# The softmax sums of layer 0 in four streams of 32 columns

## The chip, the cores and the metric

The kernel runs on one core of a Trainium2 chip. The metric is the device time of one execution in microseconds. "Before" is the median of three executions. One further execution was recorded by the hardware profiler, and every duration of a single instruction comes from that one.

The engines are named as in the profile: PE is TensorE (matmul), PEld its weight loads, DVE VectorE, ACT ScalarE, POOL GpSimd, and SP the engine whose queue issues most of the transfers. PSUM is the memory into which PE writes its results; a bank holds 512 f32 values in each of 128 partitions. SBUF is the working memory.

## What is computed

Two attention layers follow each other on `x` of shape (8, 512, 32, 32): 8 batches, 512 channels, 1024 tokens, 8 heads of 64 channels. Only layer 0 is touched. Cut to what matters:

```python
normed = group_norm(x)                                # 32 groups
q, k, v = split(qkv_w @ normed + qkv_b)               # each 8 heads x 64 x 1024
weight = einsum('bct,bcs->bts', q * scale, k * scale) # scores
weight = softmax(weight, axis=-1)
a = einsum('bts,bcs->bct', weight, v)
out = proj_w @ (normed_in + a) + proj_b
x = x + out
```

The kernel doesn't divide each weight. It takes `e = exp(scores)` and multiplies `e` with `v`, sums `e` over the keys, and multiplies the result by the reciprocal of that sum at the end. The sums are what the change is about.

## The kernel before

**How the work is cut.** The order of all instructions on all engines is written out by hand; nothing is rearranged by a scheduler, and each engine works its own list in order. Layer 0 goes through the batches one by one. For a batch, `attention0` works through 8 groups: 4 pairs of heads times 2 halves of 512 queries. A group has `NG` = 8 blocks of 128 keys, so there are 64 steps `i` for a batch.

- `scores(i)` (line 972): four 64x64 matmuls of 512 columns into a PSUM tile of two banks, then `exp` on ACT (line 977) into `e[i]`, a tile of 128 partitions by 2 x 512. The partitions are the 128 keys of the block, the middle index `m` is the head of the pair.
- `values(i)` (line 998): products of `e` with `v`, summed over the 8 blocks in two PSUM banks, tags `a0` (two buffers) and `a1`. After the last block ACT copies both to `u[g]` (line 1009).
- `sums(i)` (lines 983 and 985): DVE adds `e[i]` to `zacc[g]`, of the same shape. After the last block, `zacc[g]` still has 128 partial sums for each query and head, one in each partition.

The loop takes two steps at a time: `scores` of i and i + 1, then `values` and `sums` of i - 2 and i - 1, then what an agenda has for the slots i and i + 1. For a group whose last block has just been done, the agenda gets `totals(g)` at slot i + 2, `reciprocals(g)` at i + 6 and `finish(g)` at i + 10. Group 7 of a batch comes too late for the loop; its three steps run in `ag.flush()`, after the next batch's k projection (`qk0(b + 1, "k")`) has been issued, or at the end of the layer for the last batch.

**The steps that the change touches.**

- `totals(g)` (line 1011) adds the 128 partial sums by a matmul with a matrix of ones. It does so for the upper and the lower 64 partitions apart: half `a` goes into `z[a]`, `z[0]` in a buffer of tag `a0`, `z[1]` in the bank `small`. Each of the four matmuls is 64 rows by 64 columns and streams 512 columns. Then ACT copies `z[0]` and DVE `z[1]` to `row`, and SP issues two transfers that bring one row of each head into `zc[g]`, laid out over 128 partitions with 8 values each.
- `reciprocals(g)` (line 1031) adds the two halves of the values `u[g]`, adds the two halves of the sums into `zs` (line 1035), takes the reciprocal, writes it to a DRAM tile `zd`, and reads it back spread over 64 partitions for each head as `rzb[g]` (line 1042). It also keeps a record in `chk` for a later test of the range.
- `finish(g)` (line 1056) multiplies `u[g][0]` by `rzb[g]` (line 1058) and adds it to `xa` (line 1060), the input of the output projection.

The bank `small` has a second user: the group statistics of the next batch. `gs.means` (line 616) copies the means on DVE into `gs_m` (line 618) and multiplies them on PE into `pm` (line 620) in `small`. It is due at slot 43, directly behind `totals(4)` at slot 42; `finish(3)` is due at slot 42 too, ahead of `totals(4)`. `gs.squares` follows at slot 45 (line 631). This happens for batches 0 to 6, each preparing the next.

After the flush of group 7 come the v and q projections of the next batch (lines 846 and after), which use the `a0` buffers as well; for the last batch comes the output projection, of which the last part needs `finish(7)`.

Layer 1 has a `totals` of its own (line 1567, matmul at line 1574), which isn't changed. It sums over all 128 partitions at once, in four streams of 32 columns:

```python
nc.tensor.matmul(
    ps[c * 32 : c * 32 + 32, m].rearrange("p (g c i) -> p g c i", g=4, i=Q8),
    ones[:, :32],
    self.by_head(z[:, c // 2])[:, c % 2 * 4 : c % 2 * 4 + 4],
    start=True, stop=True, tile_position=(0, c * 32),
)
```

Of the kernel before, what the change touches and what calls it, by code (L numbers as in the profile page):

```python
# [9 lines left out]
F32 = mybir.dt.float32  # L10
# [8 lines left out]
P = 128  # L19
# [448 lines left out]
def tile_two_attention_layers(  # L468
# [19 lines left out]
    nc = tc.nc  # L488
    B, C, T = x_d.shape
    H = w_head.shape[0]  # L490
    D = C // H
    NCC = C // P
    NT = T // P
    FB = 512
# [21 lines left out]
    def const_tile(name, shape, dt=F32):  # L516
        return const.tile(shape, dt, tag=name, name=name)
# [13 lines left out]
    ones = const_tile("ones", [P, P])  # L531
# [118 lines left out]
    with ExitStack() as l0:  # L650
# [4 lines left out]
        zpool = l0.enter_context(tc.tile_pool(name="zpool", bufs=2))  # L655
        stat = l0.enter_context(tc.tile_pool(name="stat", bufs=2))
        ps_s = l0.enter_context(tc.tile_pool(name="ps_s", bufs=2, space=PSUM))
        ps_a = l0.enter_context(tc.tile_pool(name="ps_a", bufs=1, space=PSUM))

        def small_psum(nm):  # L660
            return ps_a.tile([P, FB], F32, tag="small", name=nm)

        def score_psum(nm):
            return ps_s.tile([P, 2, FB], F32, tag="s", name=nm)
# [295 lines left out]
        def attention0(b, agenda):  # L960
            q, k, v = q_t[b], k_t[b], v_t[b]
            e, acc, u, zacc, zc, rzb = {}, {}, {}, {}, {}, {}

            def scores(i):

                f, hp, kc = i // (NG * H // 2), i // NG % (H // 2), i % NG
                ps = score_psum(f"s0_{b}_{i}")
                for c in range(2):
                    for m in range(2):
                        r = slice(m * D, m * D + D)  # L970
                        k0 = kc * P + c * D
                        nc.tensor.matmul(  # L972
                            ps[c * D : c * D + D, m], k[r, hp, k0 : k0 + D], q[r, hp, ts(f, FB)],
                            start=True, stop=True,
                        )
                e[i] = epool.tile([P, 2, FB], F32, tag="e", name=f"e0_{b}_{i}")
                nc.scalar.activation(e[i], ps, AF.Exp, scale=S0 * S0)  # L977

            def sums(i):
                g, kc = i // NG, i % NG  # L980
                if kc == 1:
                    zacc[g] = zpool.tile([P, 2, FB], F32, tag="zacc", name=f"zacc_{b}_{g}")
                    nc.vector.tensor_add(zacc[g], e[i - 1], e[i])
                elif kc > 1:
                    nc.vector.tensor_add(zacc[g], zacc[g], e[i])  # L985

            def values(i):

                g, hp, kc = i // NG, i // NG % (H // 2), i % NG
                if kc == 0:  # L990
                    acc[g] = [
                        ps_a.tile([P, FB], F32, tag=f"a{a}", name=f"a0_{b}_{g}_{a}", bufs=2 - a)
                        for a in range(2)
                    ]
                for a in range(2):
                    rows = slice(a * D, a * D + D)
                    for m in range(2):
                        nc.tensor.matmul(  # L998
                            acc[g][a][m * D : m * D + D], v[rows, kc, ts(2 * hp + m, D)],
                            e[i][rows, m], start=(kc == 0), stop=(kc == NG - 1),  # L1000
                        )
                if kc == NG - 1:

                    u[g] = [
                        zpool.tile([P, FB], F32, tag=f"u{a}", name=f"u_{b}_{g}_{a}")
                        for a in range(2)
                    ]
                    for a in (1, 0):
                        nc.scalar.copy(u[g][a], acc[g][a])

            def totals(g):

                z = [
                    ps_a.tile([P, FB], F32, tag="a0", name=f"z_{b}_{g}", bufs=2),
                    small_psum(f"z_{b}_{g}_1"),
                ]
                for a in range(2):
                    rows = slice(a * D, a * D + D)
                    for m in range(2):
                        nc.tensor.matmul(  # L1020
                            z[a][m * D : m * D + D], ones[rows, :D], zacc[g][rows, m],
                            start=True, stop=True,
                        )
                row = zpool.tile([P, 2, FB], F32, tag="row", name=f"row0_{b}_{g}", bufs=1)
                nc.scalar.copy(row[:, 0], z[0])
                nc.vector.tensor_copy(row[:, 1], z[1])
                zc[g] = stat.tile([P, 2, T // P], F32, tag="zc", name=f"zc_{b}_{g}")
                for a in range(2):
                    nc.sync.dma_start(out=zc[g][:, a], in_=row[0::D, a])

            def reciprocals(g):

                nc.vector.tensor_add(u[g][0], u[g][0], u[g][1])
                zs = stat.tile([P, T // P], F32, tag="zs", name=f"zs_{b}_{g}")
                nc.vector.tensor_add(zs, zc[g][:, 0], zc[g][:, 1])
                rz = stat.tile([P, T // P], F32, tag="rz0", name=f"rz_{b}_{g}")
                nc.vector.reciprocal(rz, zs)
                zd = dram.tile([2, FB], F32, tag=f"zd0_{b}_{g}", name=f"zd0_{b}_{g}")
                nc.sync.dma_start(out=zd, in_=rz)
                rzb[g] = zpool.tile([P, FB], F32, tag="rzb", name=f"rzb_{b}_{g}")  # L1040
                for m in range(2):
                    nc.sync.dma_start(
                        out=rzb[g][m * D : m * D + D], in_=zd[m].partition_broadcast(D)
                    )
                col = b * H + g
                junk = stat.tile([P, T // P], F32, tag="junk0", name=f"junkz_{b}_{g}")
                nc.vector.tensor_scalar(
                    junk, zs, 1.0, 0.0, ALU.mult, ALU.add, accum_out=chk[:, 1, col : col + 1]
                )
                r2 = stat.tile([P, T // P], F32, tag="r20", name=f"r2_{b}_{g}")  # L1050
                nc.vector.scalar_tensor_tensor(
                    r2, rz, 1.0 / RZ_MAX, rz, ALU.mult, ALU.mult,
                    accum_out=chk[:, 0, col : col + 1],
                )

            def finish(g):
                hp, f = g % (H // 2), g // (H // 2)
                nc.vector.tensor_mul(u[g][0], u[g][0], rzb[g])
                dst = xa_t[b][:, hp, ts(f, FB)]
                nc.vector.tensor_add(dst, dst, u[g][0])  # L1060


            for i in range(0, NI + 2, 2):
                if i < NI:
                    scores(i)
                    scores(i + 1)
                if i >= 2:
                    for w in (i - 2, i - 1):
                        values(w)
                        sums(w)  # L1070
                    if (i - 1) % NG == NG - 1:
                        g = (i - 1) // NG
                        agenda.at(i + 2, lambda g=g: totals(g))
                        agenda.at(i + 6, lambda g=g: reciprocals(g))
                        agenda.at(i + 10, lambda g=g: finish(g))
                agenda.run(i)
                agenda.run(i + 1)
# [55 lines left out]
    with ExitStack() as l1:  # L1133
# [8 lines left out]
        zpool = l1.enter_context(tc.tile_pool(name="zpool1", bufs=1))  # L1142
        stat = l1.enter_context(tc.tile_pool(name="stat1", bufs=2))
        gstat = l1.enter_context(tc.tile_pool(name="gstat", bufs=1))
        ps_a = l1.enter_context(tc.tile_pool(name="ps1_a", bufs=1, space=PSUM))
# [583 lines left out]
        for b in range(B):  # L1729
            more = b + 1 < B  # L1730
            a = Attention1(b)
# [105 lines left out]
```

## Time and profile before

| | us |
|---|---|
| median of three executions | 4401.87 |
| lowest, highest | 4401.12, 4406.87 |
| the profiled execution's own time | 4397.52 |
| its span in the trace | 4395.7 |
| `zacc` sums' matmul, line 1020: 512 instructions, duration of one | 0.589 |
| copy of `z[0]` on ACT, line 1025: 64, duration of one | 0.586 |
| copy of `z[1]` on DVE, line 1026: 64, duration of one | 0.692 |
| issue of a transfer `zc`, line 1029: 128, duration of one | 0.555 |
| add of the halves, line 1035: 64, duration of one | 0.160 |

A matmul on f32 data appears as two instructions in the trace, so 64 calls with four matmuls give 512. Matmuls on different parts of the array run beside each other, and their ends are modelled. So their durations can't be added up; how long a block of matmuls holds PE is read from the start of its first instruction to the start of the next block's first one. In a timeline each line has the start, the length from the first start to the last end, engine, line, operation, result and operands, sizes, and how many instructions were merged. What stands in brackets is how long the engine had been idle before, and what ended that.

Layer 0 takes the first 1,790 us or so of the span; the rest is layer 1.

### The profile page before, as it was taken

To read this page: it belongs to the slowest core of one execution; us is meant where nothing else is said; L and a number is where in the kernel's file an instruction comes from. 1 tells how busy PE (TensorE), PEld (TensorE's weight loads), DVE (VectorE), ACT (ScalarE), POOL (GpSimd) and SP (SyncE) were. 2 spreads that over 40 slices of the span, in tenths; PEclk is the share of its full clock that TensorE was granted. 3 is DMA by queue.
4 is the path that set the end of the run, shared out by engine and by line. 5 is a ranking of instruction groups with operands and counts; after the bars stand their busy time and mean duration, and the time that the engine had idled before them with its cause. 6 is when DMAs were issued, how large, how long until landed. Compare 5 with 4: busy or idle time off the path is not lost.

```text
span 4395.7 us, 131459 instructions
## 1 busy us (share of the span) xinstructions
PE 4251.2 (97%) x58752; PEld 2266.0 (52%) x58752; DVE 2690.5 (61%) x3683; ACT 2330.0 (53%) x2747; POOL 53.4 (1%) x86
## 2 busy tenths in 40 slices
PE   7999999999999999899999999999999999999998
PEld 4353535353535353366466466466466465465565
DVE  4748484848484847268367377277277277376387
ACT  1717172727272725078177177187187286286385
POOL 0000000000000000000000000000000000000000
PEclk9999999999999999899999999999999999999999
DMA  4112121211111111277186176275285384384474
GB/s 134 59 57 70 58 69 58 69 63 66 64 63 65 62 56 38 77 184 182 54 200 165 65 197 157 77 196 146 89 196 134 97 206 117 113 198 108 115 175 134
DMA packets 249311, 487.13 MB, mean 111 GB/s; under 512 B 58592, under 2 KB 63072, under 8 KB 244512
## 3 DMA queue, kind: packets, MB, share of 16 engines
q1 hardware_dynamic: 243856, 475.84, 39.2%
q8 instruction: 462, 7.57, 0.7%
q0 software_dynamic: 2576, 0.69, 0.3%
q10 hardware_dynamic: 2304, 2.10, 0.1%
q14 instruction: 113, 0.93, 0.1%
HBM read 167.53 MB, written 41.42 MB: 48 GB/s over the span
## 4 chain that ended last, share of the span: by engine, by line
PE 89%; DVE 4%; DMA 3%; ACT 2%; issue 2%; SPq 0%; DVEq 0%; ACTq 0%
PE a L1543 11%; PE s L1449 11%; PE m L1497 10%; PE s L972 9%; PE a L998 9%; PE pk L1248 5%; PE pv L1272 5%; PE pq L1304 5%; PE pp L1334 4%; PE pp_p L846 4%; PE pv_p L846 4%; PE pk_p L846 4%; PE pq_p L846 4%; PE t L1574 2%; DMA re<-raw 1%
## 5 line engine op out<-in xcount | busy, mean ns | idle before, releaser
L1497 PEld LDWEIGHTS m<-wmix,re 64*64 64x64 f32 x32768 | 581.3, 135 | 130.8 <-issue 64.2
L1497 PE MATMUL m<-wmix,re 64*64 64x64 f32 x32768 | 594.0, 219 | 32.0 <-issue 25.8
L977 ACT ACTIVATE e<-s 128x1024 f32<-128x1024 f32 x512 | 497.2, 1026 | 229.8 <-PE s L972 229.8
L1543 PE MATMUL a<-e,v 128*64 128x256 f32 x4096 | 558.8, 392 | 25.6 <-ACT q L1565 21.0
L1521 DVE TENSOR_TENSOR z<-z,e 128x1024 f32<-128x1024 f32 x448 | 537.2, 1218 | 54.5 <-ACT e L1503 54.4
L1525 DVE TENSOR_TENSOR z<-z,e 128x1024 f32<-128x1024 f32 x448 | 534.5, 1218 | 57.6 <-ACT e L1514 56.8
L1503 ACT ACTIVATE e<-m 128x1024 f32<-128x1024 f32 x512 | 528.5, 1032 | 74.3 <-PE m L1497 70.8
L1449 PE MATMUL s<-k,q 64*64 64x256 f32 x8192 | 550.6, 387 | 4.9 <-issue 4.9
L972 PE MATMUL s<-q,k 64*64 64x512 f32 x4096 | 487.5, 591 | 2.3 <-ACT e L977 2.3
L985 DVE TENSOR_TENSOR zacc<-zacc,e 128x1024 f32<-128x1024 f32 x384 | 468.0, 1219 | 26.9 <-ACT e L977 2.3
L998 PE MATMUL a<-e,v 64*64 64x512 f32 x4096 | 484.1, 589 | 0.0
L1514 ACT ACTIVATE e<-e 128x1024 f32<-128x1024 f32 x448 | 461.9, 1062 | 0.0
L1464 ACT COPY raw<-s 128x1024 f32<-128x1024 f32 x368 | 373.8, 1016 | 149.8 <-PE s L1449 118.4
L1449 PEld LDWEIGHTS s<-k,q 64*64 64x64 f32 x8192 | 268.2, 132 | 266.8 <-issue 172.8
L1543 PEld LDWEIGHTS a<-e,v 128*64 128x64 f32 x4096 | 251.1, 136 | 146.4 <-ACT q L1565 24.3
L998 PEld LDWEIGHTS a<-e,v 64*64 64x64 f32 x4096 | 156.6, 133 | 282.9 <-issue 282.9
L972 PEld LDWEIGHTS s<-q,k 64*64 64x64 f32 x4096 | 152.9, 133 | 283.2 <-issue 259.4
L1462 DVE COPY raw<-s 128x1024 f32<-128x1024 f32 x144 | 176.2, 1223 | 109.1 <-PE s L1449 98.0
L1248 PE MATMUL pk<-y,wk 128*128 128x512 f32 x512 | 230.3, 604 | 4.4 <-DMA y<-x 4.4
L1312 ACT COPY q<-pq 128x512 f32<-128x512 f32 x32 | 18.8, 586 | 396.5 <-DVE q L1314 396.5
L1272 PE MATMUL pv<-wv,y 128*128 128x512 f32 x512 | 227.6, 598 | 0.0
L1304 PE MATMUL pq<-y,wq 128*128 128x512 f32 x512 | 221.1, 592 | 0.0
(261 smaller groups left out, 3766.5 us busy)
## 6 DMA issues: line engine op xcount, KB each, us to landing
re<-raw SPq DMA_DIRECT2D x1024, 256.0 KB
x<-in_x_dram SPq DMA_DIRECT2D x32, 512.0 KB
rzb<-zd SPq DMA_DIRECT2D x128, 128.0 KB
x<-x SPq DMA_DIRECT2D x64, 256.0 KB
rzb<-zd SPq DMA_DIRECT2D x64, 256.0 KB
left_p<-left_p SPq DMA_DIRECT2D x9, 1792.0 KB
left_k<-left_k SPq DMA_DIRECT2D x8, 1792.0 KB
left_v<-left_v SPq DMA_DIRECT2D x8, 1792.0 KB
```

What stands on the lines that cost most here:

```text
L846: nc.tensor.matmul(out, st, mv, start=start, stop=(k == 1), skip_group_check=True)
L972: nc.tensor.matmul(ps[c * D : c * D + D, m], k[r, hp, k0 : k0 + D], q[r, hp, ts(f, FB)], start=True, stop=True,)
L977: nc.scalar.activation(e[i], ps, AF.Exp, scale=S0 * S0)
L985: nc.vector.tensor_add(zacc[g], zacc[g], e[i])
L998: nc.tensor.matmul(acc[g][a][m * D : m * D + D], v[rows, kc, ts(2 * hp + m, D)], e[i][rows, m], start=(kc == 0), stop=(kc == NG - 1),)
L1449: last = nc.tensor.matmul(pv[c * D : c * D + D, m, j], qo_t[b][r, 2 * qb + j, hp, ts(c, D)], k_t[b][r, hp, ts(kb, KB)], start=True, stop=True,
L1497: last = nc.tensor.matmul(ps[c * D : c * D + D, a, ts(r, D)], self.re[t, r][rows, j, k0 : k0 + D], wmix[rows].rearrange("p g i -> p (g i)" ...
L1503: nc.scalar.activation(self.e[y][:, j], ps.rearrange("p a c -> p (a c)"), AF.Exp)
L1514: nc.scalar.activation(e2, self.e[y][:, j], AF.Square)
L1521: nc.vector.tensor_add(self.z[:, j], self.z[:, j], self.e[y][:, j])
L1525: nc.vector.tensor_add(self.z2[:, j], self.z2[:, j], self.e2[j])
L1543: last = nc.tensor.matmul(self.acc[w][two * D : two * D + D, s].rearrange("p (c i) -> p c i", i=Q8), v_t[b][:, kc, ts(g, D)], e[:, g], sta ...
```

## The change

The upper and lower halves of the partitions are no longer kept apart. One matmul now takes all 128 rows, and the columns are cut instead: four matmuls, each with 32 columns of ones and 256 of the 1024 columns of `zacc`, write to four strips of 32 partitions of one bank. Strip `c` holds the sums of head `c // 2`, half `c % 2` of the 512 queries. `z` is half a bank of tag `a0`; `small` isn't used here any more. One copy on ACT brings it to `row`, now half as wide and with two buffers, and one transfer takes one row of each strip into `zc[g]`. The add of the two halves falls away, since `zc[g]` is already the full sum.

```diff
             def totals(g):
 
-                z = [
-                    ps_a.tile([P, FB], F32, tag="a0", name=f"z_{b}_{g}", bufs=2),
-                    small_psum(f"z_{b}_{g}_1"),
-                ]
-                for a in range(2):
-                    rows = slice(a * D, a * D + D)
-                    for m in range(2):
-                        nc.tensor.matmul(
-                            z[a][m * D : m * D + D], ones[rows, :D], zacc[g][rows, m],
-                            start=True, stop=True,
-                        )
-                row = zpool.tile([P, 2, FB], F32, tag="row", name=f"row0_{b}_{g}", bufs=1)
-                nc.scalar.copy(row[:, 0], z[0])
-                nc.vector.tensor_copy(row[:, 1], z[1])
-                zc[g] = stat.tile([P, 2, T // P], F32, tag="zc", name=f"zc_{b}_{g}")
-                for a in range(2):
-                    nc.sync.dma_start(out=zc[g][:, a], in_=row[0::D, a])
+
+                HB = FB // 2
+                z = ps_a.tile([P, FB], F32, tag="a0", name=f"z_{b}_{g}", bufs=2)[:, :HB]
+                for c in range(4):
+                    nc.tensor.matmul(
+                        z[c * 32 : c * 32 + 32], ones[:, :32], zacc[g][:, c // 2, ts(c % 2, HB)],
+                        start=True, stop=True, tile_position=(0, c * 32),
+                    )
+                row = zpool.tile([P, HB], F32, tag="row", name=f"row0_{b}_{g}")
+                nc.scalar.copy(row, z)
+                zc[g] = stat.tile([P, T // P], F32, tag="zc", name=f"zc_{b}_{g}")
+                nc.sync.dma_start(out=zc[g], in_=row[0::32])
 
             def reciprocals(g):
 
                 nc.vector.tensor_add(u[g][0], u[g][0], u[g][1])
-                zs = stat.tile([P, T // P], F32, tag="zs", name=f"zs_{b}_{g}")
-                nc.vector.tensor_add(zs, zc[g][:, 0], zc[g][:, 1])
+                zs = zc[g]
                 rz = stat.tile([P, T // P], F32, tag="rz0", name=f"rz_{b}_{g}")
                 nc.vector.reciprocal(rz, zs)
```

## The prediction, made before the changed kernel had run

> **What bounds the kernel now.** I read the page first (busy shares, chain that ended last), then the PE timeline around one call of `totals`, then the waits of PE and PEld over layer 0, and last the timelines of the places where those waits lie.
>
> ```profile
> span 4395.7 us, 131459 instructions
> PE 4251.2 (97%) x58752; PEld 2266.0 (52%) x58752; DVE 2690.5 (61%) x3683; ACT 2330.0 (53%) x2747; POOL 53.4 (1%) x86
> ...
> PE 89%; DVE 4%; DMA 3%; ACT 2%; issue 2%; SPq 0%; DVEq 0%; ACTq 0%
> ```
>
> TensorE is the bound: 97% busy and 89% of the chain, so an edit is worth what it does to the spacing of matmuls, and work taken from DVE, ACT or SP is worth something only where PE waits for it. Next, PE alone, around one `totals` (start, length, line, instructions merged):
>
> ```profile
> 558.48 1.90 PE L998 MATMUL a<-e,v 64*64 64x512 f32 x16
> 560.20 1.04 PE L1020 MATMUL z<-zacc,ones 64*64 64x512 f32 x8
> 561.06 1.90 PE L972 MATMUL s<-q,k 64*64 64x512 f32 x16
> 562.77 1.90 PE L998 MATMUL a<-e,v 64*64 64x512 f32 x16
> ```
>
> Lengths overlap (ends are modelled), so I read starts. Sixteen instructions take 561.06 to 562.77, 1.72 us: each f32 matmul is two instructions and four 64x64 ones run side by side, so one wave of four with 512 columns takes 0.43 us. The sums are two waves, 560.20 to 561.06, 0.86 us, with no gap before or after. They really occupy PE.
>
> The nearest thing to the new form is in layer 1, line 1574: all 128 rows, 32 columns, four streams.
>
> ```profile
> 1945.80 1.08 PE L1543 MATMUL a<-e,v 128*64 128x256 f32 x8
> 1946.82 1.92 PE L1574 MATMUL t<-z,ones 128*32 128x512 f32 x16
> 1948.67 1.09 PE L1449 MATMUL s<-k,q 64*64 64x256 f32 x16
> 1949.58 0.63 PE L1497 MATMUL m<-wmix,re 64*64 64x64 f32 x30
> ```
>
> Sixteen instructions in 1.85 us are four waves of 0.43 (1.72) plus 0.13 for changing the shape; so four 32-column streams do run side by side. The 64x64 block after them takes 0.91 us for four waves of 256 columns; at half of 0.43 these are 0.86, so its first wave is 0.05 late.
>
> The waits of PE and PEld in layer 0 name few places. One recurs seven times, where the group statistics of the next batch come right after `totals(4)`:
>
> ```profile
> 400.89 0.69 DVE L1058 TENSOR_TENSOR u<-u,rzb 128x512 f32<-128x512 f32 x1 [1.06 <-DMA rzb<-zd]
> 401.61 0.69 DVE L1060 TENSOR_TENSOR xa<-xa,u 128x512 f32<-128x512 f32 x1
> 401.68 1.04 PE L1020 MATMUL z<-zacc,ones 64*64 64x512 f32 x8
> 402.81 0.69 DVE L1026 COPY row<-z 128x512 f32<-128x512 f32 x1 [0.51 <-PE z L1020]
> 403.42 0.16 DVE L618 COPY gs_m<-mv 128x4 f32<-128x4 f32 x1
> 403.72 0.36 PE L620 MATMUL pm<-gs_m,gavg 128*128 128x4 f32 x2 [1.01 <-DVE gs_m L618]
> ```
>
> The reader is to see a circle through DVE: PE finishes z, DVE evicts half of it, only then copies gs_m, and PE waits for gs_m. From z to pm are 2.04 us instead of about 0.9. The other place is the end of layer 0, where the last `totals` heads a serial chain:
>
> ```profile
> 1745.59 0.59 ACT L1025 COPY row<-z 128x512 f32<-128x512 f32 x1 [0.96 <-ACT u L1009]
> ...
> 1748.24 0.68 DVE L1026 COPY row<-z 128x512 f32<-128x512 f32 x1
> 1748.84 0.68 DVE L1033 TENSOR_TENSOR u<-u,u 128x512 f32<-128x512 f32 x1
> ...
> 1750.91 0.17 DVE L1035 TENSOR_TENSOR zs<-zc 128x8 f32<-128x8 f32 x1 [1.39 <-DMA zc<-row]
> ...
> 1760.01 6.18 PE L846 MATMUL pp_p<-tmp_xa,left_p 128*128 128x512 f32 x8 [7.43 <-DVE tmp_xa L826]
> ```
>
> The DVE copy is late (DVE stood on the previous group's rzb), its transfer lands 2 us later, and PE is idle for 7.43 us at the end of that chain.
>
> **What the skill says.** The Trainium skill, "TensorEngine Tiling (Array Packing)", Key Properties: changing the tiling mode drains TensorE. The trace agrees: the 32 instructions of line 998 before a 128x128 product run from 221.99 to 225.53, 3.54 us where two blocks of 1.72 are 3.43, 0.11 more. The skill's "TensorE: Matmul & The Clock Gate", Part 3, has outputs of few columns in different column groups run at the same time; line 1574 agrees (four in 0.43). Its Part 1 has the clock halve after an idle window of about 3.4 us; the windows view gives PEclk 0.50 for 1754.8 to 1765.0, in that 7.43 us hole.
>
> **The change part by part.** There are 64 calls of `totals`: 49 between values and scores, 7 followed by pm (group 4 of batches 0 to 6), 8 in the flush at each batch's end (group 7).
>
> *A, PE in the 49 plain calls.* Instructions stay 8, waves stay 2, each of 256 columns: 2 x 0.215 = 0.43. New are two changes of shape (64x64 to 128x32 and back): 0.10 before z (the 0.11 of line 998), 0.13 in z's own block (the excess of line 1574), 0.05 in the scores behind it. Together 0.71 against 0.86: 0.15 gained, x49 = 7.3 us. The bounds: if the excesses count double in part, 0.62, 12 us; if all is eaten by draining, 0. That loading weights for 256-column waves could limit is excluded by line 1497, where waves of 64 columns go every 0.07 us.
>
> *B, the seven calls before pm.* DVE has no copy to wait for, so gs_m runs straight after xa. In the place shown xa ends at 402.30, gs_m by 402.4, pm follows about 0.3 after gs_m starts (403.42 to 403.72): 402.5 instead of 403.72, 1.2 gained. PE itself would be ready at 401.68 + 0.10 + 0.56 = 402.34. In four others (184.80, 836.99, 1053.87, 1270.76) xa ends early enough and PE decides: pm at 0.66 after the old start of z instead of 2.04, 1.38 gained each. In two (618.57, 1487.65) rzb landed late, finish still holds DVE, and the gain is 0.6 each. Sum 5.5 + 1.2 + 1.2 = 7.9 us. What is late next is finish's own wait for rzb, which stays. Further on, line 631 waits for DVE steps that had over 1 us to spare; they move up as well. Bounds 5 (rzb late in more of them) to 9.6.
>
> *C, seven flushes.* z starts when DVE's k write frees its bank (249.96) and still does. Then 0.56 instead of 1.02, but the v product behind it needs the second k write, done at 250.62 and felt at about 250.68 instead of 250.98: 0.3 each, 2.1 us.
>
> *D, the last flush.* Only ACT's copy and one transfer lead to zc: copy done by about 1745.6, landed some 2 us later, before 1748. DVE then decides: without its copy, u+u ends near 1748.9 and the reciprocal starts there instead of at 1751.11: 2.2 us off the 7.43 hole. The hole stays longer than a clock window, so the half-clock stretch after it (10.2 us, of which some 5 are matmuls) may shift by a window either way: bounds 0.5 to 5; I take 2.2.
>
> *At nothing.* ACT's copy shrinks from 586 ns to perhaps 370 (the 64x256 copy of line 1565 takes 366; bounds 300 and 586): hidden, as ACT had waited 105.1 us for z before those copies. DVE loses 44.1 us of copies and 10.3 us of zs adds, hidden behind PE outside B and D. SP loses 64 issues of 0.56 us and the wait for DVE's copy; what stands behind it (x loads, zd, rzb) can only move up, and PE's list of waits in layer 0 holds no DMA. If these covers were gone they would gain, not cost. No wait is added: z keeps its a0 bank and rotation, the small bank loses a user, row gets a second buffer. Layer 1's code is the same; it starts earlier.
>
> **Sum.** 7.3 + 7.9 + 2.1 + 2.2 = 19.5 us. The profiled execution took 4397.5 us (span 4395.7), so 4378.0; the three timed runs have a median of 4401.9, 4.4 above it, and their spread is 5.8. Carried to that median: 4382.4; I say 4382.
>
> **Rivals.**
> 1. *The shape changes eat A.* For it: each first wave after a change is late, and waves are now half as long. Against: the excesses above. A = 0: 4389.7.
> 2. *B does not come*, because finish's rzb holds DVE in all seven. For it: 48 of the 64 finishes wait for rzb. Against: four places with DVE free before z ends. B near 1: 4389.
> 3. *Slower: the four full-height streams do not run side by side on these operands* (place: every z block in layer 0). Eight instructions of 0.215 one after another are 1.72, with the changes 2.0 instead of 0.86: 49 x 1.14 = 56, flushes 7 x 0.8 = 5.6, B falls to about nothing, D stays 2.2: plus 59, 4461. It decides once a plain block costs over 1.11 us (12.2 us of B, C and D spread over 49 calls), as two-by-two would. Against: line 1574, the same shape.
> 4. *No change:* layer 1, whose PE waits for transfers in places, gives back by chance what layer 0 gains: about 4400.
>
> **How the numbers follow.** Forecast 0.72, rival 1 0.12, rival 2 0.07, rival 3 0.05, rival 4 0.04. The forecast's own range from the bounds: gains of 11 to 27 us, 4374 to 4391; with A at its top and the clock in D 4370, with rivals 1 and 2 and the runs' spread 4395. What a measurement can tell from no change is some 0.2%, 9 us, so up to 4393 is faster. Rivals 1 and 2 lie 12 us down and count three quarters as faster, one quarter as same; with rival 4: faster 0.87, same 0.08, slower 0.05.
>
> **What would show it.** PE's timeline: z to scores 0.55 to 0.6, values' last block 0.1 longer; pm 0.6 to 1.0 after z's start; no DVE copy of row; the hole before the last projection near 5.2 us; layer 1 as long as before. Wrong: a z block over 0.86, or pm still waiting over 1 us, or a total within 5 us of before.

## The result and the profile after

The changed kernel took 4375.1 us in the median of four executions (4372.5 to 4379.6), the kernel before 4403.6 (4401.1 to 4406.9). The ratio is 0.9936, with a 95% interval from 0.9919 to 0.9953. The forecast was 4382, its range 4370 to 4395. It is faster as forecast, and the gain is larger: 28.5 us by the medians and 25.1 by the spans of the two profiled executions, where the sum had 19.5.

The page of the changed kernel, same lines as before:

```profile
span 4370.6 us, 131167 instructions
...
PE 4239.7 (97%) x58752; PEld 2253.6 (52%) x58752; DVE 2642.4 (60%) x3555; ACT 2316.1 (53%) x2747; POOL 53.5 (1%) x86
...
PE 92%; DVE 3%; DMA 2%; ACT 1%; issue 1%; SPq 0%; POOL 0%; DVEq 0%; ACTq 0%; POOLq 0%
```

PE is still the bound. Its busy time fell by only 11.5 us while the span fell by 25.1: about half of the gain is waiting that went away, which shares of busy time don't show. DVE lost 48 us, most of which lay beside PE.

The places come out of the starts of PE's blocks in both traces. From the first score to the first matmul of layer 1, layer 0 takes 1683.4 us before and 1659.1 after:

| part of layer 0 | forecast | measured |
|---|---|---|
| A, 49 plain calls of `totals` | 7.3 | 49 x 0.129 = 6.3 |
| B, seven calls ahead of pm | 7.9 | 11.0 |
| C, seven flushes | 2.1 | 2.1 |
| D, the end of layer 0 | 2.2 | 4.9 |
| sum | 19.5 | 24.3 |

The rest of the 25.1 is no work of the change: the first score came 2.2 us earlier after the same start-up code (over all twelve traces of this study it starts anywhere from 104.4 to 107.4 us), and layer 1 took 1.4 us more.

A plain call, PE's timeline of the changed kernel (start, length, line, instructions merged):

```profile
780.34 1.90 PE L998 MATMUL a<-e,v 64*64 64x512 f32 x16
782.17 0.64 PE L1017 MATMUL z<-zacc,ones 128*32 128x256 f32 x8
782.74 1.95 PE L972 MATMUL s<-q,k 64*64 64x512 f32 x16
784.51 1.90 PE L998 MATMUL a<-e,v 64*64 64x512 f32 x16
```

By starts: the values before z hold PE for 1.83 in place of 1.72, z for 0.57, the scores behind for 1.77 in place of 1.72. So a call costs 0.73 where it had cost 0.86. In every plain call of the trace these three numbers are the same to 2 ns.

The call ahead of pm, all engines, same batch as the one shown before:

```profile
395.11 0.69 DVE L1052 TENSOR_TENSOR u<-u,rzb 128x512 f32<-128x512 f32 x1 [1.17 <-DMA rzb<-zd]
395.83 0.69 DVE L1054 TENSOR_TENSOR xa<-xa,u 128x512 f32<-128x512 f32 x1
396.44 0.16 DVE L618 COPY gs_m<-mv 128x4 f32<-128x4 f32 x1
...
396.62 0.64 PE L1017 MATMUL z<-zacc,ones 128*32 128x256 f32 x8
...
397.19 0.39 PE L620 MATMUL pm<-gs_m,gavg 128*128 128x4 f32 x2
397.32 0.37 ACT L1022 COPY row<-z 128x256 f32<-128x256 f32 x1 [1.08 <-PE z L1017]
```

gs_m now leaves before z has even started, and pm follows z without a wait (0.57 after its start, in place of 2.05). It does so in all seven batches, also in the two in which it had been held to 2.16 and 3.58. From the values before z to the values behind pm, five batches gain 1.34 us each and these two 1.45 and 2.87.

The end of layer 0 after the change:

```profile
1721.69 0.64 PE L1017 MATMUL z<-zacc,ones 128*32 128x256 f32 x8
...
1722.81 0.39 ACT L1022 COPY row<-z 128x256 f32<-128x256 f32 x1
...
1723.33 0.69 DVE L1052 TENSOR_TENSOR u<-u,rzb 128x512 f32<-128x512 f32 x1 [2.18 <-DMA rzb<-zd]
...
1725.27 0.19 DVE L1031 RECIPROCAL rz<-zc 128x8 f32<-128x8 f32 x1
...
1734.23 2.28 PE L846 MATMUL pp_p<-tmp_xa,left_p 128*128 128x512 f32 x3 [4.12 <-DVE tmp_xa L826]
```

The reciprocal comes 3.6 us after the start of z instead of 6.7, and PE's hole (the stretch in which it is idle) shrinks from 7.43 to 4.12 us.

### The profile page after: what moved, and what is told of

It is laid out like the page before. It is cut to its first block, busy times and chain, and to the rows that moved or that the text cites. A ratio compares the mean times of both kernels' runs of the same rounds, so it can differ in the third digit from the quotient of the medians.

```text
span 4370.6 us, 131167 instructions
## 1 busy us (share of the span) xinstructions
PE 4239.7 (97%) x58752; PEld 2253.6 (52%) x58752; DVE 2642.4 (60%) x3555; ACT 2316.1 (53%) x2747; POOL 53.5 (1%) x86
## 4 chain that ended last, share of the span: by engine, by line
PE 92%; DVE 3%; DMA 2%; ACT 1%; issue 1%; SPq 0%; POOL 0%; DVEq 0%; ACTq 0%; POOLq 0%
PE a L1537 11%; PE s L1443 11%; PE m L1491 11%; PE s L972 10%; PE a L998 10%; PE pk L1242 5%; PE pv L1266 5%; PE pq L1298 5%; PE pp L1328 4%; PE pp_p L846 4%; PE pv_p L846 4%; PE pk_p L846 4%; PE pq_p L846 4%; PE t L1568 2%; ACT q L1559 1%
## 5 line engine op out<-in xcount | busy, mean ns | idle before, releaser
L1537 PEld LDWEIGHTS a<-e,v 128*64 128x64 f32 x4096 | 250.9, 136 | 145.3 <-ACT q L1559 24.3
```

What stands on the lines that cost most here:

```text
L1537: last = nc.tensor.matmul(self.acc[w][two * D : two * D + D, s].rearrange("p (c i) -> p c i", i=Q8), v_t[b][:, kc, ts(g, D)], e[:, g], sta ...
```

## The experiments

The question was which part of the edit pays for what: the form of the matmul (A), the order on DVE, the bank shared with pm, or the number of transfers; and then why B and D were larger than the sum. Where an experiment's verdict lies inside layer 0, the length of layer 0 from first score to layer 1 is given: it is 1659.1 and 1659.3 us in two profiled executions of the changed kernel, while layer 1, whose code is the same in all kernels here, ranged from 2593 to 2614 us over all traces.

**1. The form of the matmul undone.** Everything else of the change stays, but `z` and `row` are 512 columns wide again.

```diff
-                HB = FB // 2
-                z = ps_a.tile([P, FB], F32, tag="a0", name=f"z_{b}_{g}", bufs=2)[:, :HB]
-                for c in range(4):
+                z = ps_a.tile([P, FB], F32, tag="a0", name=f"z_{b}_{g}", bufs=2)
+                for m in range(2):
                     nc.tensor.matmul(
-                        z[c * 32 : c * 32 + 32], ones[:, :32], zacc[g][:, c // 2, ts(c % 2, HB)],
-                        start=True, stop=True, tile_position=(0, c * 32),
+                        z[m * D : m * D + D], ones[:, :D], zacc[g][:, m],
+                        start=True, stop=True,
                     )
-                row = zpool.tile([P, HB], F32, tag="row", name=f"row0_{b}_{g}")
+                row = zpool.tile([P, FB], F32, tag="row", name=f"row0_{b}_{g}")
...
-                nc.sync.dma_start(out=zc[g], in_=row[0::32])
+                nc.sync.dma_start(out=zc[g], in_=row[0::D])
```

> All of the change except the form of the matmul: two streams of 64 columns over all 128 rows with 512 columns each, one bank, one copy on ACT, one transfer, no add of halves. Theory (how long the sums hold PE is a part of its own): a plain block takes 0.86 us plus the changes of shape, some 0.42 more per call than with four streams, 49 plain calls 20.6, the calls before pm 3, the flushes 2: 26 us over the changed kernel, about 4401, no gain left over the kernel before. Rival (the gain is the copy, the bank and the transfer; the form of the matmul is neutral): 4375, as the changed kernel.

Measured: 4398.3 us, ratio to before 0.9997 (0.9990 to 1.0003). PE's timeline:

```profile
341.02 1.90 PE L998 MATMUL a<-e,v 64*64 64x512 f32 x16
342.84 1.08 PE L1016 MATMUL z<-zacc,ones 128*64 128x512 f32 x4
343.85 1.95 PE L972 MATMUL s<-q,k 64*64 64x512 f32 x16
```

z holds PE for 1.01 us instead of 0.57, with half the instructions: what counts is how many columns are streamed one after another. Layer 0 takes 1686.0, 26.9 more than in the changed kernel, where the theory had 26. The rival falls. One bank, one copy and one transfer alone would have brought no time at all: the form that they need (all rows in one matmul) costs, with two streams, as much as they gain, and layer 0 is even 2.6 us longer than before.

**2. The kernel before, with pm moved away from `totals`.**

```diff
-            agenda.at(slot + 23, gs.means)
-            agenda.at(slot + 25, gs.squares)
-            agenda.at(slot + 27, scale)
+            agenda.at(slot + 24, gs.means)
+            agenda.at(slot + 26, gs.squares)
+            agenda.at(slot + 28, scale)
...
-                    ag.at(49 + 4 * c, lambda c=c: normalize0(b + 1, c))
+                    ag.at(50 + 4 * c, lambda c=c: normalize0(b + 1, c))
```

> The kernel before with the group statistics of the next batch one slot later (means at slot 44, squares at 46, scale at 48, the normalisations at 50, 54, 58, 62), so that pm no longer follows totals(4) directly; totals is that of before. Theory (the copy on DVE with gs_m queued behind it held PE): the seven waits of 1.2 to 2.7 us go, pm then pays its own change of shape of 0.1, a gain of 8 to 9.5 us, about 4394. Rival (pm waits for something else, or the wait is hidden): 4403, no gain.

Measured: 4394.7 us, ratio 0.9985 (0.9977 to 0.9992), some 6.6 us; layer 0 takes 1676.4, 7.0 less than before. In the batch shown throughout:

```profile
403.10 0.16 DVE L618 COPY gs_m<-mv 128x4 f32<-128x4 f32 x1
...
403.40 0.36 PE L620 MATMUL pm<-gs_m,gavg 128*128 128x4 f32 x2
403.69 1.52 PE L972 MATMUL s<-q,k 64*64 64x512 f32 x12
```

The wait was real and on the path. The gain is short of the 8 to 9.5 expected, because in five batches PE still waits 0.1 us for gs_m, and in the two with a late rzb 0.7 and 1.4. So moving pm cures the circle, but not the lateness of `finish`, which no longer reaches pm in the changed kernel.

**3. The one copy put back on DVE.**

```diff
-                nc.scalar.copy(row, z)
+                nc.vector.tensor_copy(row, z)
```

> The changed kernel with the one copy of z on DVE in place of ACT; all else the same. Theory (DVE order): gs_m queues behind the copy again, pm some 1.35 us after the start of z in place of 0.57, 7 x 0.75 = 5 us; at the end of layer 0 DVE falls behind again, 1 to 4 us; 4381 to 4384. Rival (it was the bank small, shared by z and pm, that held PE): 4375.

Measured: 4387.4 us, ratio 0.9969 (0.9957 to 0.9981). All seven calls look like this one:

```profile
397.90 0.64 PE L1017 MATMUL z<-zacc,ones 128*32 128x256 f32 x8
398.61 0.42 DVE L1022 COPY row<-z 128x256 f32<-128x256 f32 x1 [0.31 <-PE z L1017]
398.95 0.16 DVE L618 COPY gs_m<-mv 128x4 f32<-128x4 f32 x1
...
399.17 0.39 PE L620 MATMUL pm<-gs_m,gavg 128*128 128x4 f32 x2 [0.62 <-DVE gs_m L618]
```

The bank `small` isn't used by z here, and pm still waits 0.69 us longer than in the changed kernel: the order on DVE is a wait of its own. At the end of layer 0 another line stands:

```profile
1734.04 2.92 PE L846 MATMUL pp_p<-xa,left_p 128*128 128x512 f32 x3 [5.51 <-DVE row L1022]
```

The copy stands behind `finish(6)`, which waits for its rzb, and the output projection can't start because its second `a0` bank is still z's. Layer 0 takes 1667.5, 8.4 more than in the changed kernel (5.2 up to the last batch, 3.2 at the end); the two effects had been expected to make 6 to 9. The time itself lies above the 4381 to 4384 expected: by the ratios to before, this kernel is some 14 us slower than the changed one. The profile puts 4.7 of that into layer 1, and what is left can't be told from chance.

**4. The kernel before, with both copies on ACT.**

```diff
-                nc.vector.tensor_copy(row[:, 1], z[1])
+                nc.scalar.copy(row[:, 1], z[1])
```

> The kernel before with the copy of z[1] on ACT as well; two banks, two transfers, the matmuls as before. Theory (DVE in arrears after its wait for z; and separately the bank small, which z[1] and pm share): gs_m leaves before z starts and the reciprocal of group 3 comes some 6.3 to 6.5 us after z(3) in place of 8.1 to 10.8, but pm now waits for the second copy on ACT, which ends at about 0.43 + 0.65 + 1.1 us after the start of z: pm 2.2 to 2.4 us after it in all seven, so nothing gained there; the last z no longer waits for zacc, and the hole at the end of layer 0 is near 5 us in place of 7.4. Rival (the order on DVE alone held pm): pm about 1 us after z.

One execution: 4400.5 us. The call ahead of pm:

```profile
400.08 1.04 PE L1020 MATMUL z<-zacc,ones 64*64 64x512 f32 x8
400.30 0.16 DVE L618 COPY gs_m<-mv 128x4 f32<-128x4 f32 x1
...
401.64 0.59 ACT L1026 COPY row<-z 128x512 f32<-128x512 f32 x1
...
402.28 0.38 PE L620 MATMUL pm<-gs_m,gavg 128*128 128x4 f32 x2 [1.16 <-ACT row L1026]
```

gs_m is done, and pm waits for ACT to empty the bank: 2.20 after the start of z in all seven. So there had been two waits in one place, of which the profile named only the later one. A cure for DVE alone, with the bank kept, brings nothing at pm in six of the seven batches; only the one that had been held to 3.58 gains. It does shorten the end of layer 0 (160.3 us from the start of the last batch to layer 1, against 163.6 before and 157.8 after). The reciprocal of group 3 came 7.5 to 8.2 us after z(3), not at the 6.3 to 6.5 expected: DVE gets there only after 7.3 us, and then waits 0.2 to 0.9 us for zc.

**5. The bank shared again.**

```diff
-                z = ps_a.tile([P, FB], F32, tag="a0", name=f"z_{b}_{g}", bufs=2)[:, :HB]
+                z = small_psum(f"z_{b}_{g}")[:, :HB]
```

> The changed kernel with z in the bank small in place of a buffer of a0. Theory (the shared bank is a wait of its own): pm waits for the end of ACT's copy of z, which starts 0.70 after z and takes 0.37: pm 1.15 us after the start of z in place of 0.57 in all seven. In the flushes z need not wait for the k write (0.72 from the last k wave in place becomes 0.54) but the v product still does. Rival (only DVE's order mattered): pm stays at 0.57.

One execution: 4377.0 us.

```profile
396.87 0.16 DVE L618 COPY gs_m<-mv 128x4 f32<-128x4 f32 x1
...
397.25 0.37 ACT L1022 COPY row<-z 128x256 f32<-128x256 f32 x1 [1.08 <-PE z L1017]
...
397.68 0.39 PE L620 MATMUL pm<-gs_m,gavg 128*128 128x4 f32 x2 [0.49 <-ACT row L1022]
```

pm starts 1.13 after z (1.15 expected) in all seven, and layer 0 takes 1661.6. The bank is the second wait, shown alone: 7 x 0.56 = 3.9 us. Layer 0 is only 2.4 longer. The flushes gain 0.34 each, 2.4 in sum: z starts there without waiting for the k write, as expected, but the v product then follows without a wait too (0.57 after z in place of 0.71), which was not. The end of layer 0 is 0.9 longer in this one execution.

**6. Two transfers instead of one.**

```diff
-                nc.sync.dma_start(out=zc[g], in_=row[0::32])
+                for m in range(2):
+                    rows = slice(m * D, m * D + D)
+                    nc.sync.dma_start(out=zc[g][rows], in_=row[rows][0::32])
```

> The changed kernel with zc brought by two transfers of two strips each, both issued after ACT's copy. Theory (the number of transfers is off the path): the second lands some 0.6 us after the first, still before DVE comes to the reciprocal (6.2 to 6.4 us after z in the plain case), so PE's gaps in layer 0 stay: pm 0.57 after z, layer 0 as long as in the changed kernel within 1 us. Rival (one transfer fewer is a part of the gain): reciprocals of group 3 later than 7 us after z(3), pm held in some batches, the hole at the end longer by 0.6 or more.

One execution: 4376.5 us. pm stays at 0.57 in six batches and comes at 0.93 in one; layer 0 takes 1661.7, 2.6 more than in the changed kernel, 1.9 of it at its end, where the hole is 4.69 us in place of 4.12. That is more than the 1 us allowed by the theory, and close to the 0.6 us of the hole that the rival had named. In the batch with 0.93, rzb was issued 2.9 us after zd, where 1.4 is usual: a late landing. What lies at the end can't be told from chance in one execution, so a share of up to 2 us for the saved transfer stays open. It is not where the gain came from.

**7. The changed kernel once more.**

> The changed kernel once more, to compare with the kernel before in the same session and with the pairs: 4371 to 4375, a ratio near 0.993. If the run of the pairs was better by its own merit and not by chance, this one stays some 4 to 10 us above it.

Measured: 4378.1 us beside 4405.8 before, ratio 0.9939 (0.9925 to 0.9953). The time is 3 us above what was expected, the ratio as expected.

**8. The sums of two groups in one block.** Three pairs of groups of a batch are summed together, so that two calls share the changes of shape. `zacc` and `u` get a third buffer, and the first group of a pair is divided a group later.

```diff
-            def totals(g):
+            def totals(gs):
...
+                z = ps_a.tile([P, 2, HB], F32, tag="a0", name=f"z_{b}_{gs[0]}", bufs=2)[:, :n]
+                for j, g in enumerate(gs):
+                    for c in range(4):
+                        nc.tensor.matmul(
+                            z[c * 32 : c * 32 + 32, j], ones[:, :32],
+                            zacc[g][:, c // 2, ts(c % 2, HB)],
+                            start=True, stop=True, tile_position=(0, c * 32),
+                        )
...
+                        if g in (1, 3, 5):
+                            agenda.at(i + 2, lambda g=g: totals([g - 1, g]))
+                            agenda.at(i + 6, lambda g=g: reciprocals(g - 1))
+                            agenda.at(i + 8, lambda g=g: reciprocals(g))
+                            agenda.at(i + 10, lambda g=g: finish(g - 1))
+                            agenda.at(i + 12, lambda g=g: finish(g))
```

> The changed kernel with the sums of groups 0 and 1, 2 and 3, 4 and 5 taken in one block of sixteen instructions (one bank, one copy, two transfers), groups 6 and 7 alone. Theory (a call costs 0.43 of streams and 0.30 of changes of shape): a pair costs 1.16 in place of 2 x 0.73, 24 pairs gain 7 us, pm alone pays 1 more: 4369. Rival (the changes of shape cost nothing of their own, the four waves as much as before): 4375, or more if the later reciprocals are felt.

> The pairs once more. From the blocks seen (1.16 for a pair with its neighbours, 0.73 for one call) and the length of layer 0 from the first score to layer 1 (1655.4 against 1659.2 in the changed kernel) it should be 4 us ahead of the changed kernel, a ratio to the kernel before of 0.992 to 0.993; the 0.9908 of the first time holds some chance from layer 1. If it is again near 0.991, something outside layer 0's blocks belongs to it.

Measured: 4362.5 us, ratio 0.9908 (0.9892 to 0.9923), and the second time 4366.2, ratio 0.9918 (0.9904 to 0.9931).

```profile
195.25 1.90 PE L998 MATMUL a<-e,v 64*64 64x512 f32 x16
197.07 1.07 PE L1019 MATMUL z<-zacc,ones 128*32 128x256 f32 x16
198.08 1.95 PE L972 MATMUL s<-q,k 64*64 64x512 f32 x16
199.84 1.90 PE L998 MATMUL a<-e,v 64*64 64x512 f32 x16
```

By starts, values 1.82, z 1.01, scores 1.76: with the 0.11 and 0.05 at its sides a pair costs 1.16 or 1.17, as expected, so a call's 0.73 is 0.43 of streams and 0.30 of changes of shape. Layer 0 takes 1655.4 in both profiled executions, 3.7 to 3.9 less than in the changed kernel. That is short of the 6 of the theory, more than half of it at the end of layer 0, which is 0.2 to 0.4 longer where the theory had 0.9 shorter. The ratios say some 9 to 12 us less; that part of it which layer 0 doesn't hold belongs to the spread of layer 1 as far as these traces show.

**9. Pairs placed so that one stands ahead of pm** (groups 1 and 2, 3 and 4, 5 and 6).

> Pairs of groups 1 and 2, 3 and 4, 5 and 6, groups 0 and 7 alone, so that the block of 3 and 4 stands at slot 42, directly ahead of pm, and shares a change of shape with it; reciprocals and finishes of a pair in neighbouring slots. Theory: pm without its own way in and out, 7 x 0.2 = 1.4 us off the pairs' layer 0: 1654. Rival: the later reciprocals of group 6 hold DVE in the flush, and layer 0 is longer than with the first pairs.

Measured: 4364.0 us, ratio 0.9908 (0.9893 to 0.9923); layer 0 takes 1655.7, no better than the first pairs. Up to the last batch it is 0.8 us shorter, and the end of layer 0 is 1.2 longer: the reciprocal of group 6 comes later there, and `finish(6)`, which waits for its rzb, starts 2.8 us after the last z in place of 1.6. Both versions with pairs are faster than the kernel before. Against the changed kernel they are shorter in layer 0, while the intervals of the ratios still touch.

## Why the prediction came out as it did

- **A, right, 1 us too large.** The excesses were read from other changes of shape, one in layer 0 and two in layer 1: 0.10, 0.13 and 0.05 were forecast, and 0.11, 0.14 and 0.05 came. Experiment 1 shows that the half-length waves carry this part, experiment 8 that the changes of shape are a price per visit.
- **B, right in kind, 7.9 forecast and 11.0 measured, above its upper bound of 9.6.** Nearly all of the excess lies in the two batches with a late rzb: 2.87 and 1.45 came where 0.6 each was forecast. The step that failed is "What is late next is finish's own wait for rzb, which stays." In four of the seven batches that wait is gone (at most 0.02 us), and in the others (0.4 to 1.2 us) it ends too early to hold pm. DVE before, around the reciprocal of group 3:

```profile
388.22 0.69 DVE L1026 COPY row<-z 128x512 f32<-128x512 f32 x1 [0.88 <-PE z L1020]
388.83 5.21 DVE L985 TENSOR_TENSOR zacc<-zacc,e 128x1024 f32<-128x1024 f32 x4
...
395.62 0.17 DVE L1035 TENSOR_TENSOR zs<-zc 128x8 f32<-128x8 f32 x1 [0.91 <-DMA zc<-row]
```

and the same stretch after:

```profile
382.34 2.54 DVE L985 TENSOR_TENSOR zacc<-zacc,e 128x1024 f32<-128x1024 f32 x2
385.24 2.55 DVE L985 TENSOR_TENSOR zacc<-zacc,e 128x1024 f32<-128x1024 f32 x2 [0.36 <-ACT e L977]
...
389.80 0.20 DVE L1031 RECIPROCAL rz<-zc 128x8 f32<-128x8 f32 x1 [1.33 <-DMA left_v<-left_v]
```

Before, DVE stood 0.88 us waiting for z, copied for 0.69, and then had four additions to do back to back: it was in arrears (behind with its list) for the rest of the group. After, it reaches the additions early enough to wait for ACT. Without the wait for zc that stands in brackets, DVE would have come to the reciprocal of group 3 7.8 to 8.1 us after z(3) before, and 6.2 to 6.3 after. How much of this is the copy, experiments 3 and 4 show in group 6, where in most batches DVE waits for no transfer at this place: the reciprocal comes at 7.7 before and at 6.4 with the copy on ACT (experiment 4), at 5.9 after and at 6.8 with the copy back on DVE (experiment 3).

The wait for zc came on top, 0.3 to 2.9 us in all seven batches before; after, four batches have none. It has a second cause, in SP's list. Between rzb of group 2 and zc of group 3, SP issues the loads of the next batch's weights. In the batch that was held longest, before:

```profile
597.69 0.33 SPq L1039 DMA_DIRECT2D zd<-rz  x1
600.43 1.13 SPq L1042 DMA_DIRECT2D rzb<-zd  x2
601.61 0.57 SPq L696 DMA_DIRECT2D left_k<-left_k  x1
602.28 0.38 SPq L696 DMA_DIRECT2D left_v<-left_v  x1
606.46 1.25 SPq L1029 DMA_DIRECT2D zc<-row  x2
...
614.60 0.17 DVE L1035 TENSOR_TENSOR zs<-zc 128x8 f32<-128x8 f32 x1 [2.87 <-DMA zc<-row]
```

From zd to rzb it took 2.7 us here, where 1.4 is usual, and the loads left 1.7 us later than usual. Wherever DVE waits for zc of group 3 in the two traces, the wait ends 11.4 to 13.0 us after `left_k` was issued, and in the line of the reciprocal shown above the profile itself names `left_v`. An earlier reciprocal of group 2 lets the loads out earlier too: in undisturbed batches 4.1 us ahead of z(3) before, and 5.6 to 5.7 after. This link is read from the traces; no run moved the loads, and why zd is sometimes late stays open.

In those seven batches, both together: the reciprocal of group 3 came 8.1 to 10.8 us after z(3) before and 6.2 to 7.7 after (in the repeat of the changed kernel 8.1 in one batch). `finish(3)` had ended up to 2.8 us after the start of z(4), and after the change it ends 0.1 to 1.4 us ahead of it, so that it holds gs_m in no batch. A late zd came after the change as well (3.2 us in one batch) and was covered; experiment 6 shows one, of group 3 itself, that wasn't. So 1.6 us of the 11.0 hang on two late landings in the trace of the kernel before. Experiment 2 keeps the old `totals` and keeps the lateness (8.1 to 10.7): a late rzb there still holds pm in the same two batches.
- **The two waits in B.** The prediction took the bank `small` for free with the rest ("the small bank loses a user"). Experiments 4 and 5 show it as a wait by itself, worth 3.9 us once DVE's is gone.
- **C, right:** the v product starts 0.71 us after z in place of 1.02, the k write deciding.
- **D, right in kind, 2.2 forecast and 4.9 measured, just inside its bounds.** The mis-sized term is "u+u ends near 1748.9 and the reciprocal starts there", 4.5 us after the last z: it kept `finish(6)` and z where they had been. The same arrears went. Before, z itself had waited for DVE:

```profile
1744.42 1.09 PE L1020 MATMUL z<-zacc,ones 64*64 64x512 f32 x8 [0.97 <-DVE zacc L985]
```

After, z doesn't wait, `finish(6)` starts 1.6 us after it in place of 2.5, and the reciprocal comes at 3.6. The hole is 3.3 shorter (4.12), and PEclk stands at 0.50 for 3.4 us where it had been 10.2 (5.0 of these behind the hole), worth 0.8. In return the projection behind z waits 0.65 us for ACT. Experiment 3 brings part of the loss back.
- **At nothing,** right for ACT (copies of 0.373 us). For SP it is open up to 2 us (experiment 6). DVE's 48 us were entered as hidden "outside B and D"; they were hidden as busy time, but their place in DVE's order cost more than B and D said.
- **The rivals.** 1, 2 and 3 are excluded by the blocks: A came to 6.3 us, pm's wait went in all seven, and four streams of full height run side by side. Of 4, layer 1 gave back 1.4 us in this pair of traces; its spread of 21 us over all traces is what limits how well any single total here can be known.
- **The range.** The gains of 11 to 27 us that it names are not the sum of the parts' bounds, which is 7.6 to 28.7; the 24.3 us measured in layer 0 lie in both.

## What to carry to other kernels

When an instruction leaves an in-order engine, don't only take away its own time and the wait of the one behind it. Follow that engine's list to the next result that someone else waits for, and ask whether the engine was in arrears until there: here a copy of 0.69 us, which first waited for PE, delayed a reciprocal four additions later by 1.3 us (7.7 against 6.4 in experiment 4), and through two transfers a matmul. And where a wait has been read from a profile, look for the second holder of the same instruction (an order and a bank here): each alone kept pm waiting, 1.26 and 1.13 us after z in place of 0.57.

## What had not been expected of the hardware

A change of the array's shape cost the same for two waves as for four (0.30 us in and out together), and a wave of four full-height streams of 256 columns took 0.216 us, per column within 1% of the 64x64 waves (0.429 us for 512); the first wave after a change took 0.240. Layer 1, with the same code in all twelve traces, took between 2593 and 2614 us.
